# A gated cross-attention block on one Trainium2 core: the added rows of the last unit of the first two down parts stored from GpSimd's queue

## Chip, core and metric

The kernel runs on one core of one Trainium2 chip. The metric is the device time of one execution in microseconds (us); lower is better. Every launch includes all weight preparation.

## What is computed

The reference is a gated Flamingo layer in float32 on 2048 tokens (16 sequences of 128) of width 1024: a cross attention with 32 query heads and 8 key/value heads, then a gated feed-forward of hidden width 2752, each added to the stream behind a tanh gate.

```python
x = x + tanh(g_xattn[0]) * attention(layernorm(x), ctx, ctx, Wq, Wk, Wv, Wo)
h = layernorm(x).reshape(-1, 1024)
y = (silu(h @ W_gate.T) * (h @ W_up.T)) @ W_down.T
x = x + tanh(g_ffn[0]) * y
```

The change lies in the last line: the down projection and its addition to the stream.

## The kernel before

**Products.** Every float32 operand is split into a high and a low part (`split`, lines 112 to 115: a cast on ScalarE, a subtraction on VectorE), and a product is three matmuls for each slice of 128 of the inner dimension: high by high, high by low, low by high. A 2 by 2 block product is done with seven products of half size instead of eight. `still` (line 656) makes the sums of the stationary blocks and splits them into tiles `sta`, `stb`, `stc`, `std`; `premake`, `swap` and `casts` make the seven moving operands `m1` to `m7` (each a high tile such as `m1h` and a low tile such as `m1l`) from the weight.

**Down parts and units.** The hidden dimension of the down projection is done in three parts of 8, 8 and 6 tiles of 128 (`CHUNKS`). `Down(c, p)` is one unit: part `c`, 256 tokens number `p`, so 8 units a part and 24 in all. A unit runs the products in `ORDER = (1, 5, 6, 2, 7, 3, 4)`. Products 1, 6, 7 and 4 add up in one PSUM bank, and after each of them VectorE adds the bank to a row tile `c` (line 851), so TensorE may not write the next of them into the bank before VectorE has read the last.

**Row tiles.** A unit has four row tiles of 128 by 512, 256 KB each. `fetch` loads one from `x1d`, the stream kept in device memory, through ScalarE's queue (line 843), two products ahead of the product that first adds to it (1, 5, 6 and 4). After products 2, 7, 3 and 4 the row tile is complete and is stored (line 854): to `x1d` in the first two parts, to the output in the third. The tiles turn over in five buffers: a fetch can be issued only when the store that last used its buffer has landed. So the fetch for product 5 of a unit waits for the first store of the unit before it, the fetch for product 6 for the second, for product 4 for the third, and the fetch for product 1 of the unit after that for the fourth. ScalarE works in order: a fetch that waits holds the casts behind it.

**The turn of a part.** `swap` puts steps around the last unit of a part, unit 7, to bring in the next part's moving operands. In unit 7, after product 1 it splits `m1` and starts a weight load, after product 5 it splits `m5`, after product 6 it loads `m6` ready made (`bring`, line 962, two loads of 1 MB, `m6h` and `m6l`), and after product 4 it loads `m4` the same way. In unit 0 of the next part it splits `m2` after product 1, `m7` after product 5 and `m3` after product 6. In units 0 and 1 of each part the sums of `still` run on VectorE, in the others on GpSimd.

**Queues.** The program's order on each engine is the order in which Python emits it (a manual schedule). All loads and stores around the turn but the fetches go through SyncE's queue, one after another in order; GpSimd issues DMAs only for additions into memory (lines 922 and 1007), before the down parts. At the turn SyncE's order is: the weight load, `m6h`, `m6l`, the four stores of unit 7, `m4h`, `m4l`, and the load of hidden rows `raw` for two units ahead.

Of the kernel before, what the change touches and what calls it, by code (L numbers as in the profile page):

```python
# [17 lines left out]
P = 128  # L18
NTOK = 2048
# [17 lines left out]
CHUNKS = (range(0, 8), range(8, 16), range(16, 22))  # L37
# [17 lines left out]
def flamingo_kernel(ctx: ExitStack, tc: tile.TileContext, x, ctxt, gx, gf, wqkv, wo, wgu, wge, wd, out):  # L55
# [9 lines left out]
    nc = tc.nc  # L65
# [36 lines left out]
    od, rd, x1d = ([None] * (NTOK // P) for _ in range(3))  # L102
# [616 lines left out]
    class Gated:  # L719
# [22 lines left out]
        def done(self, p, ps, cols):  # L742
            c = self.c
            tt = nc.vector.tensor_tensor
            if p in (1, 5, 6):
                i = {1: 1, 5: 3, 6: 2}[p]
                if cols in (ALL, MOST):
                    self.room(i)
                nc.scalar.copy(c[i][:, cols], ps)  # L749
            elif p == 2:  # L750
                tt(c[1], ps, c[1], ALU.add)  # L751
            elif p == 7:
                tt(c[3][:, cols], c[3][:, cols], ps, ALU.subtract)
            elif p == 3:
                tt(c[2], ps, c[2], ALU.subtract)
                if self.amid:
                    self.amid()
                nc.scalar.activation(c[1], c[1], AF.Silu)
                nc.scalar.activation(c[2], c[2], AF.Silu)
                tt(c[2], c[2], c[3], ALU.mult)  # L760
                keep_hidden(self.g, self.f, c[2], 1)
            else:
                tt(c[1], ps, c[1], ALU.mult)
                keep_hidden(self.g, self.f, c[1], 0)
# [48 lines left out]
    class Down:  # L813
# [34 lines left out]
        def done(self, p, ps, _):  # L848
            y = self.y[self.PLACE[p]]
            g = tg[:, 2:3] if p in self.MINUS else tg[:, 1:2]  # L850
            nc.vector.scalar_tensor_tensor(y, ps, g, y, ALU.mult, ALU.add)  # L851
            if p in self.LAST:
                b, cols = self.row(p)
                nc.sync.dma_start(out[ts(b, P), cols] if self.c == len(CHUNKS) - 1 else x1d[b][:, cols], y)

    def run(units, cb, ready, steps, edge):

# [362 lines left out]
```

## Time and profile before

| | |
|---|---|
| median of 4 runs | 1839.84 us (1839.51 to 1842.57) |
| profiled execution | 1839.57 us |
| its span, first to last instruction | 1837.7 us |
| TensorE matmul busy | 1817.1 us, 99% of the span |
| VectorE / ScalarE / GpSimd busy | 1210.3 / 900.2 / 545.4 us |
| mean granted TensorE clock | 0.998 |
| line 854, stores to `x1d` | 64 of 256 KB |
| line 843, fetches from `x1d` | 96 of 256 KB |

The span is shorter than the execution by 1.9 us of start and end. In the profile, PE is TensorE, DVE is VectorE, ACT is ScalarE, POOL is GpSimd, SP is SyncE, and a "q" behind the name (SPq, ACTq, POOLq) is the engine's issuing of DMAs. The DMA queue q1 is SyncE's, q10 ScalarE's and q0 GpSimd's. The down parts run from about 1413 us to the end; the two turns that the change touches are near 1560 and 1715 us.

### The profile page before, as it was taken

What the parts mean: (1) busy time and instruction counts of PE and PEld (TensorE: products, weight loads), DVE (VectorE), ACT (ScalarE), POOL (GpSimd) and SP (SyncE); (2) the same over time, 40 slices, a digit from 0 to 9 for tenths busy, and PEclk for the clock granted to TensorE, in tenths of its full rate; (3) what the DMA queues carried; (4) which work ended last, traced back from release to release, by engine and by line L of the source; (5) the groups of instructions that cost most, each with busy time, mean ns of one, the idle gap of its engine ahead of it and who ended that gap; (6) DMA issues with size and microseconds to landing.
All of it is one profiled execution on the core that took longest, in us unless ns stands there. A gap on an engine that the chain in (4) does not pass through costs nothing.

```text
span 1837.7 us, 23463 instructions
## 1 busy us (share of the span) xinstructions
PE 1817.1 (99%) x8296; PEld 1493.4 (81%) x8296; DVE 1210.3 (66%) x1551; ACT 900.2 (49%) x1301; POOL 545.4 (30%) x372
## 2 busy tenths in 40 slices
PE   8999999999999999999999999999999999999999
PEld 7887877888887777787888888888888888788887
DVE  6757878678877777776668646355456646745765
ACT  4457787445678777776434434333334212312321
POOL 1136566221233333331021333244330231122021
PEclk9999999999999999999999999999999999999999
DMA  8699999774555445543674565675667566665764
GB/s 329 210 274 287 288 283 271 244 261 129 156 147 151 147 144 146 148 138 118 225 251 155 150 200 189 189 206 179 161 210 263 199 230 210 234 216 180 259 201 156
DMA packets 232565, 373.55 MB, mean 203 GB/s; under 512 B 38016, under 2 KB 124288, under 8 KB 227328
## 3 DMA queue, kind: packets, MB, share of 16 engines
q1 hardware_dynamic: 210400, 333.77, 55.3%
q10 hardware_dynamic: 14112, 25.17, 4.5%
q0 software_dynamic: 7936, 13.11, 4.4%
q8 instruction: 66, 1.08, 0.2%
q14 instruction: 51, 0.42, 0.1%
HBM read 247.99 MB, written 122.42 MB: 202 GB/s over the span
## 4 chain that ended last, share of the span: by engine, by line
PE 86%; DMA 5%; DVE 4%; ACT 2%; issue 1%; SPq 1%; POOL 0%; ACTq 0%; DVEq 0%; POOLq 0%
PE bx L707 35%; PE bz L707 17%; PE by L707 8%; PE bz L124 3%; PE bz L122 3%; PE bz L123 3%; PE bx L123 3%; PE bx L124 3%; PE bx L122 3%; DMA od<-os 2%; PE av L501 1%; PE av L500 1%; DMA qs<-qd 1%; PE by L472 1%; PE sc L472 1%
## 5 line engine op out<-in xcount | busy, mean ns | idle before, releaser
L483 POOL PARTITION_ALL_REDUCE mx<-pr x128 | 275.3, 2150 | 344.9 <-ACT pr L481 162.9
L674 POOL TENSOR_TENSOR sum<-raw 128x512 f32<-128x512 f32 (+1 forms) x37 | 48.0, 1297 | 479.4 <-DVE stc L115 479.4
L114 ACT CAST sta<-raw 128x1024 fp32r<-128x1024 f32 (+1 forms) x66 | 67.7, 1026 | 241.0 <-PE by L707 232.7
L707 PE MATMUL bz<-m5h,stb 128*128 128x512 f32 (+1 forms) x528 | 169.9, 383 | 0.0
L707 PE MATMUL bx<-m6h,stb 128*128 128x512 f32 (+1 forms) x528 | 169.6, 383 | 0.0
L707 PE MATMUL bx<-m7h,stc 128*128 128x512 f32 x512 | 168.9, 390 | 0.7 <-DVE c L851 0.7
L707 PE MATMUL bx<-m4h,std 128*128 128x512 f32 x512 | 169.0, 390 | 0.4 <-DVE c L851 0.4
L707 PE MATMUL by<-m2h,sta 128*128 128x512 f32 x512 | 168.5, 389 | 0.0
L707 PE MATMUL bz<-m3h,stc 128*128 128x512 f32 x512 | 168.5, 389 | 0.0
L707 PE MATMUL bx<-m1h,sta 128*128 128x512 f32 x512 | 168.4, 389 | 0.0
L751 DVE TENSOR_TENSOR c<-by,c 128x512 f32<-128x512 f32 x42 | 28.9, 687 | 144.1 <-issue 137.6
L144 POOL TENSOR_TENSOR rs__143<-ve,mhalf 128x1 f32<-128x1 f32 x32 | 29.3, 914 | 310.4 <-DVE nm L142 301.1
L495 DVE TENSOR_TENSOR pl<-pr,ph 128x512 fp32r<-128x512 f32 x128 | 120.1, 938 | 1.3 <-PE av L501 1.3
L851 DVE SCALAR_TENSOR_TENSOR c<-bx,tg,c 128x512 f32<-128x512 f32 x96 | 72.0, 750 | 66.8 <-PE bx L707 63.0
L707 PEld LDWEIGHTS bx<-m6h,stb 128*128 128x128 f32 x528 | 98.4, 188 | 20.1 <-ACT c L749 0.2
L707 PEld LDWEIGHTS bz<-m5h,stb 128*128 128x128 f32 x528 | 98.2, 188 | 20.2 <-DVE stb L115 0.5
L707 PEld LDWEIGHTS bx<-m4h,std 128*128 128x128 f32 x512 | 96.1, 188 | 22.2 <-DVE c L851 1.2
L707 PEld LDWEIGHTS bx<-m7h,stc 128*128 128x128 f32 x512 | 96.1, 188 | 22.0 <-issue 1.2
L707 PEld LDWEIGHTS by<-m2h,sta 128*128 128x128 f32 x512 | 96.1, 188 | 20.5
L707 PEld LDWEIGHTS bx<-m1h,sta 128*128 128x128 f32 x512 | 96.1, 188 | 20.4
L707 PEld LDWEIGHTS bz<-m3h,stc 128*128 128x128 f32 x512 | 96.1, 188 | 20.1
L486 DVE TENSOR_TENSOR pr<-pr,mx 128x512 f32<-128x512 f32 x128 | 87.6, 684 | 36.9 <-POOL mx L483 36.6
(400 smaller groups left out, 4636.7 us busy)
## 6 DMA issues: line engine op xcount, KB each, us to landing
raw<-in_wgu SPq DMA_DIRECT2D x42, 1024.0 KB, 6.5
x1d<-c SPq DMA_DIRECT2D x96, 256.0 KB, 2.8
c<-x1d ACTq DMA_DIRECT2D x96, 256.0 KB, 3.0
hd<-c SPq DMA_DIRECT2D x86, 256.0 KB, 2.2
od<-os SPq DMA_DIRECT2D x128, 160.0 KB, 4.1
qd<-e SPq DMA_DIRECT2D x32, 512.0 KB, 5.5
qs<-qd SPq DMA_DIRECT2D x64, 256.0 KB, 4.6
raw<-od SPq DMA_DIRECT2D x32, 512.0 KB, 5.2
```

The source lines that it names most:

```text
L114: nc.scalar.copy(h, src)
L122: nc.tensor.matmul(ps, lh, rh, start=first, stop=False)
L123: nc.tensor.matmul(ps, lh, rl, start=False, stop=False)
L124: nc.tensor.matmul(ps, ll, rh, start=False, stop=last)
L144: nc.gpsimd.tensor_tensor(rs, ve, mhalf, ALU.pow)
L472: nc.tensor.matmul(ss[n], ks[m][:, j, :], qs[m][:, ts(j, G)], start=True, stop=True)
L483: nc.gpsimd.partition_all_reduce(mx[n], pr[n], P, bass_isa.ReduceOp.max)
L486: nc.vector.tensor_tensor(pr[n], pr[n], mx.pop(n), ALU.subtract)
L495: nc.vector.tensor_tensor(pl[n], pr.pop(n), f32(ph[n]), ALU.subtract)
L674: lambda: tt(s1, a[1][0], a[1][1], sub),
L707: nc.tensor.matmul(ps, l_, r_, start=start and k == i == 0, stop=k == n - 1 and i == 2, skip_group_check=not start)
L851: nc.vector.scalar_tensor_tensor(y, ps, g, y, ALU.mult, ALU.add)
```

## The change

The four stores of unit 7 in the first and in the second part (8 of the 64 stores to `x1d`) are issued by GpSimd instead of SyncE. Nothing else is edited.

```diff
             if p in self.LAST:
                 b, cols = self.row(p)
-                nc.sync.dma_start(out[ts(b, P), cols] if self.c == len(CHUNKS) - 1 else x1d[b][:, cols], y)
+                final = self.c == len(CHUNKS) - 1
+                turn = self.p == NTOK // (2 * P) - 1 and not final
+                queue = nc.gpsimd if turn else nc.sync
+                queue.dma_start(out[ts(b, P), cols] if final else x1d[b][:, cols], y)
```

SyncE's order at a turn becomes: the weight load, `m6h`, `m6l`, `m4h`, `m4l`, `raw`. GpSimd gets four DMA instructions between the sums for unit 7 and the sums for unit 2 of the next part. The order on TensorE, VectorE and ScalarE is the same; the two fetches that wait for the first two stores now wait for GpSimd's transfers.

## The prediction

> **What bounds the kernel.** I read the page first, then the chain that ended last around the two turns, each engine's timeline there, and the DMA queues stretch by stretch.
>
> ```profile
> span 1837.7 us, 23463 instructions
> PE 86%; DMA 5%; DVE 4%; ACT 2%; issue 1%; SPq 1%; POOL 0%; ACTq 0%; DVEq 0%; POOLq 0%
> ```
>
> TensorE carries 86% of the chain. In the down parts it is nearly all of it, so a store can only matter where the chain leaves TensorE. The first turn is such a place. The chain there (start, us, what):
>
> ```profile
> 1554.58 2.73 PE by L707 x12
> ...
> 1557.34 0.76 DVE c L851
> ...
> 1558.11 8.74 DMA x1d<-c
> ...
> 1567.30 0.50 ACT std L114
> ...
> 1567.85 5.73 DMA c<-x1d
> 1573.57 2.20 DVE m7l L115
> ...
> 1582.91 5.78 PE bx L707 x24
> ```
>
> The first store of unit 7 takes 8.74 us to land. Until then ScalarE cannot issue the fetch for product 5 of the next unit (1566.88), and behind that fetch stand the `std` cast, the fetch for product 6 (1567.85) and the cast of `m2h` (1568.68). VectorE runs late, and TensorE's timeline shows what that costs:
>
> ```profile
> 1577.02 0.47 PE L707 MATMUL bx<-m7h,stc 128*128 128x512 f32 x1 [0.66 <-DVE c L851]
> 1582.91 0.50 PE L707 MATMUL bx<-m4h,std 128*128 128x512 f32 x1 [0.17 <-DVE c L851]
> ```
>
> How much is at stake follows from the pace. A product of a part of 8 tiles takes 2.72 us (12 matmuls). Product 2 of unit 7 starts at 1554.42, and product 4 of the next unit is ten products later: 1554.42 + 27.20 = 1581.62. It starts at 1582.91, so the first turn loses 1.29 us. At the second turn product 2 starts at 1708.20; four products of 2.72 and six of 2.04 (9 matmuls) give 1731.32, the row says 1731.70: 0.38 us. All that this change can remove is 1.67 us.
>
> **The change, part by part.** *SyncE's issues.* Eight issues of 0.32 us leave SyncE. Its own time is hidden (TensorE never waits for it here), but its order matters, on SyncE's timeline:
>
> ```profile
> 1554.61 0.32 SPq L962 DMA_DIRECT2D m6h<-m6d  x1
> 1554.98 0.42 SPq L962 DMA_DIRECT2D m6l<-m6d  x1
> 1558.11 8.90 SPq L854 DMA_DIRECT2D x1d<-c  x4
> 1567.06 0.42 SPq L962 DMA_DIRECT2D m4h<-m4d  x1
> ```
>
> The loads of `m4` stood behind the fourth store, whose addition on VectorE ends at 1566.66. Now they wait for their buffer alone, that is for the last matmul of product 4 (1565.09 plus 0.39): `m4h` goes out near 1565.6, 1.5 us earlier. At the second turn it is 1719.3 instead of 1720.43. Nobody gains: `m4` is first used at 1582.91, and `m4l`, issued at 1567.54, landed 9.2 us later, at 1576.7. But 2 MB of loads now stand ahead of fetches that were ahead of them or level. `raw` still waits for VectorE's `std` (1568.64) and goes out as before.
>
> *GpSimd's issues.* Four DMA instructions a turn. GpSimd's own rows give 1.27 to 1.30 us each for line 922 and 1.28 to 1.59 for line 1007, so 5 to 6 us a turn. They are free: GpSimd idles 54.46 us before the sums at 1587.12 and 48.67 us before those at 1735.11, and the last of the four can go out at 1566.7. Without that cover the sums would slip by some 5 us. The third and fourth stores release fetches issued at 1576.52 and 1581.22, ten and more us on, so those two cost nothing. The rows stored are read again a whole part later.
>
> *When the first store lands.* This decides. GpSimd has no plain store in the trace, so I bound it. The nearest of its transfers in size is one of 256 KB with nothing beside it, an addition in place:
>
> ```profile
> q<-q POOLq DMA_DIRECT2D x1, 256.0 KB, 4.7
> x1d<-c SPq DMA_DIRECT2D x1, 256.0 KB, 2.3
> ```
>
> Its 4.7 us against 2.3 us for a store from SyncE puts GpSimd's path at most 2.4 us longer. At the turn, though, neither row applies, since 2 MB of `m6` are in flight. What a queue of its own is worth there is shown by ScalarE's fetch issued at 1557.48: it was alone on q10 and took 8.4 us, hardly less than the store on q1. From 1557 to 1560 q10 moved nothing at all; then the queues took turns packet by packet. From 1562 to 1564:
>
> ```profile
> q1 hardware_dynamic: 65, 0.42, 67.5%
> q10 hardware_dynamic: 71, 0.15, 19.3%
> ```
>
> (packets, MB, share.) Packets are about equal, bytes are not: q1's are mostly 8 KB, the fetch's 2 KB. A third queue should get the same turns once `m6h` has passed. The lower end for the landing is 4.7 us (1562.8), the upper 8.74 + 2.4 = 11.1 us (1569.2). I take the 8.4 us of the fetch, the nearest row, because it shares instant, size and backlog: landing at 1566.5, 0.35 us earlier than now.
>
> The Trainium skill ("DMA: Bandwidth & Descriptors", section "Issuing engines are not separate DMA queues") says that DMAs of all engines run on the same 16 DMA engines and that spreading them only saves sequencer time. The 8.4 against 8.7 us agree in effect, and by that rule the change brings nothing. The same page (section "Queues, rings and completion order") has each DMA engine go round the queues packet by packet; the 71 against 65 packets agree, the empty q10 of the first 2.5 us does not, and no run here shows yet which of the two GpSimd's queue follows. By the second rule alone the store would land several us earlier and the 1.29 us of the first turn would go.
>
> *The fetch for product 5, first turn.* It is issued when the store lands, now near 1566.5 and behind `m4h` (1565.6) instead of ahead of it (1567.06). Ahead of it, it landed in 4.1 us; the fetch for product 6, issued at 1567.85 behind `m4h` and `m4l`, took 8.2 us. These are the bounds: 1570.6 and 1574.7. VectorE needs it at 1572.83. Only part of what delayed the row of 8.2 us applies (it also had the other fetch ahead of it), so I take the middle, 6.2 us: 1572.7, no cost and no gain. The ends: if the store lands before `m4h` is issued, the fetch goes out first, ScalarE and VectorE run some 1.5 us earlier and the whole 1.29 us go; if it lands no earlier than now and the fetch takes 8.2 us, it is there at 1575.1, VectorE's chain of `m7l`, product 6 and `m3l` (only 0.35 us of idle time in it) shifts by up to 2.25 us, and TensorE with it.
>
> *The second turn.* The first store landed in 5.4 us (issued at 1711.90) and is not on the chain: VectorE works without a gap from 1721.99 to 1731.6, started by TensorE's product 1. With 0.3 us less or up to 2.4 us more it lands by 1719.7. A fetch issued then has 3.9 us until VectorE's addition at 1723.66; the rows of this turn give 3.0 to 5.4 us, so its cost is 0 up to about 1 us. I take 0, and the 0.38 us stay.
>
> *Sum.* 1839.57 (profiled execution; span 1837.7 and 1.9 us around it) + 0 + 0 = 1839.6 us; 0.3 us under the median of 1839.84. Ends of this case: 1839.57 - 1.29 = 1838.3 and 1839.57 + 2.25 = 1841.8.
>
> **Rivals.** *The wait goes.* GpSimd's queue gets its turns at once, the store lands by 1565, the fetch passes ahead of `m4h`: 1838.3 us. For it: equal packets on q1 and q10. Against it: q10's silent start with 2 MB outstanding.
>
> *The store lands later than now.* The longer way through GpSimd adds to the backlog instead of hiding in it. With 11.1 us the store lands at 1569.2, 2.35 us later; the fetch goes out behind both loads of `m4` and, at 8.2 us, lands at 1577.4, 4.6 us after VectorE needs it. With 7.8 us at the second turn it is there at 1719.7 and, at 4.8 us (a fetch at 1727.58, beside the `m4` loads), lands 0.85 us late. Together 5.5 us: 1845.0 us. It decides from about 9.9 us for the landing at the first turn (9.9 - 8.74 + 2.25 = 3.4, plus some 0.3 at the second), where the loss passes 3.7 us. For it: GpSimd's 1 MB additions took up to 11.5 us, and one issued at 1106.28 amid other traffic 11.3 us. Against it: an addition reads its target too, and is four times the size.
>
> *The store's queue is no matter.* If the fetch still beats the loads, nothing changes: 1839.6 us, inside the forecast's range.
>
> **How the numbers follow.** The bound for a difference is 0.2%, 3.7 us, about what a measurement of this kernel can tell from no change. Forecast with its bounds (the indifferent queue included) 0.52; the wait goes 0.18; the store lands later 0.27, of which a tenth or so stays under 3.7 us; a gain over 3.7 us has no place in this profile, since both turns together lose 1.67 us, and gets 0.03 from the rest for what I cannot see. So faster 0.03, same 0.73, slower 0.24. The likeliest range is 1838.3 to 1841.8; for 8 in 10 it reaches down to 1837.9 (the whole 1.67 us) and up to the late store, 1845.0.
>
> **What would show it.** Right: the first `x1d<-c` of unit 7 on POOLq landing 7.5 to 9 us after VectorE's addition, `m4h` issued near 1565.6, the fetch for product 5 in 5 to 7 us, TensorE's product 4 of the next unit within 1 us of 28.5 us after product 2 of unit 7, no change at the second turn. Wrong: a landing under 6 us (gain) or over 10 us (loss), a wait of ScalarE of over 5 us ahead of `std`, or any move of TensorE away from the turns, for which I have no mechanism.

## The result and the profile after

| | median (lowest to highest) | runs |
|---|---|---|
| before | 1840.04 us (1835.69 to 1844.42) | 56 |
| after | 1842.62 us (1839.01 to 1846.87) | 36 |

The ratio is 1.0015, with a 95% interval of 1.0009 to 1.002: slower by about 2.6 us (1.7 to 3.7). That is under the 0.2% taken as the bound for one comparison, but with this many runs it stands clear of no change. The forecast was no change, 1839.6 us; the median lies 0.8 us above its likeliest range.

The profiled execution of after is one of the quickest (1839.04 us), so its span says nothing of the loss: it came to the first turn 2.5 us ahead of the profiled execution of before (product 2 of unit 7 starts at 1551.94 instead of 1554.42), and gave most of that back at the two turns. So I read each turn by itself. Its loss is the time from product 2 of unit 7 to product 1 of unit 1 of the next part, less the pace: 11 products of 2.72 us at the first turn (29.92), four of 2.72 and seven of 2.04 at the second (25.16). "+x" below means x us after the start of that product 2.

| | first turn | second turn |
|---|---|---|
| loss before | 1.46 us | 0.52 us |
| loss after | 2.89 us | 1.09 us |

The page of after, shares of the chain that ended last:

```profile
span 1837.3 us, 23467 instructions
...
PE 87%; DMA 5%; DVE 2%; ACT 2%; issue 2%; SPq 1%; POOL 0%; ACTq 0%; POOLq 0%; DVEq 0%
```

At this scale little moves. The chain of waits of after, around the first turn (start, us, what):

```profile
1559.04 5.55 DMA x1d<-c
1564.59 0.02 issue
1564.61 10.36 DMA c<-x1d
...
1575.09 0.10 DVE c L851
...
1575.76 2.28 DVE m3l L115
...
1581.88 5.75 PE bx L707 x24
```

Before, the chain went through the first store, of 8.74 us, and then the fetch for product 6 (its piece of 5.73 us in that chain is not the whole transfer, which took 8.2 us). Now it goes through the second store, of 5.55 us, and the same fetch, of 10.36 us. The store that the chain passes through is shorter, and the fetch is longer. Four timelines show why. First GpSimd, the two stores that release fetches:

```profile
1555.91 0.64 POOL L857 DMA_DIRECT2D x1d<-c  x1 [25.74 <-DMA q<-in_wd]
1559.04 0.55 POOL L857 DMA_DIRECT2D x1d<-c  x1 [2.49 <-DVE c L851]
```

Each issue takes 0.55 to 0.64 us and stands behind 2.4 us of idle or more. Then SyncE:

```profile
1552.13 0.32 SPq L965 DMA_DIRECT2D m6h<-m6d  x1
1552.50 0.42 SPq L965 DMA_DIRECT2D m6l<-m6d  x1
1563.03 0.32 SPq L965 DMA_DIRECT2D m4h<-m4d  x1
1563.40 0.43 SPq L965 DMA_DIRECT2D m4l<-m4d  x1
```

`m4h` goes out at +11.09 instead of +12.64, held only by TensorE's product 4. Then ScalarE, the fetches for products 5 and 6:

```profile
1563.47 0.33 ACTq L843 DMA_DIRECT2D c<-x1d  x1
...
1564.61 0.33 ACTq L843 DMA_DIRECT2D c<-x1d  x1
```

They go out 0.93 and 0.76 us earlier than before (+11.53 and +12.67 against +12.46 and +13.43), but now the first of them is 0.44 us behind `m4h`. What each transfer took, from the DMA issues (KB, us from issue to landing), the store first:

```profile
x1d<-c POOLq DMA_DIRECT2D x1, 256.0 KB, 7.5
...
c<-x1d ACTq DMA_DIRECT2D x1, 256.0 KB, 8.3
```

In before the same two took 8.74 and 4.1 us. The store gained 1.2 us, the fetch for product 5 lost 4.2. The fetch for product 6 stands behind it on ScalarE's queue: q10 moved 144 packets, one fetch's worth, from 1564.40 to 1570.52, and the other 144 from then to 1574.70. It took 10.4 us where before it took 8.2, the row of after first:

```profile
c<-x1d ACTq DMA_DIRECT2D x1, 256.0 KB, 10.4
...
c<-x1d ACTq DMA_DIRECT2D x1, 256.0 KB, 8.2
```

VectorE waits for the first with the addition of product 5, then for the second with the addition of product 6:

```profile
1571.91 0.75 DVE L851 SCALAR_TENSOR_TENSOR c<-bz,tg,c 128x512 f32<-128x512 f32 x1 [2.71 <-DMA c<-x1d]
...
1575.09 0.75 DVE L851 SCALAR_TENSOR_TENSOR c<-bx,tg,c 128x512 f32<-128x512 f32 x1 [0.23 <-DMA c<-x1d]
```

In before it came to the first addition without a wait, and earlier to the second:

```profile
1572.83 0.75 DVE L851 SCALAR_TENSOR_TENSOR c<-bz,tg,c 128x512 f32<-128x512 f32 x1
...
1576.12 0.75 DVE L851 SCALAR_TENSOR_TENSOR c<-bx,tg,c 128x512 f32<-128x512 f32 x1 [0.35 <-issue]
```

That wait of 0.35 us is put down to "issue", but it ends 0.08 us after the fetch for product 6 landed (1567.85 and 8.19 us). And TensorE waits for VectorE, in after:

```profile
1575.99 0.47 PE L707 MATMUL bx<-m7h,stc 128*128 128x512 f32 x1 [2.11 <-DVE c L851]
...
1581.88 0.50 PE L707 MATMUL bx<-m4h,std 128*128 128x512 f32 x1 [0.17 <-DVE c L851]
```

The idle time ahead of product 7 is 2.11 us where it was 0.66; the 1.45 us between them are the growth of the loss, 2.89 - 1.46 = 1.43. Both fetches have a part in it. The one for product 6 ended last: it landed at +23.03 instead of +21.62, 1.41 us later. But VectorE, held up by the one for product 5, was free only 0.23 us before that; with the old landing of product 6 it would still have come to that addition 1.2 us later than before (+22.92 against +21.70).

At the second turn the chain of waits of after goes through a weight load:

```profile
1718.59 7.55 DMA m4l<-m4d
1726.17 1.75 DVE m3l L115
...
1731.23 4.37 PE bx L707 x18
```

That step is put down to `m4l`, but VectorE's own row ahead of `m3l` names the fetch for product 6:

```profile
1725.50 0.75 DVE L851 SCALAR_TENSOR_TENSOR c<-bx,tg,c 128x512 f32<-128x512 f32 x1 [0.48 <-DMA c<-x1d]
```

This fetch went out at 1718.36, 0.14 us behind `m4h` (1718.22), and took 7.0 us. In before it was a microsecond ahead of `m4h` (+11.22 against +12.23) and took 3.0 us.

### The profile page after: what moved, and what is told of

Its sections match the earlier page's. It is cut to its first block, busy times and chain, and to the rows that moved or that the text cites. A ratio compares the mean times of both kernels' runs of the same rounds, so it can differ in the third digit from the quotient of the medians.

```text
span 1837.3 us, 23467 instructions
## 1 busy us (share of the span) xinstructions
PE 1814.5 (99%) x8296; PEld 1490.9 (81%) x8296; DVE 1211.8 (66%) x1551; ACT 900.5 (49%) x1301; POOL 551.8 (30%) x380
## 4 chain that ended last, share of the span: by engine, by line
PE 87%; DMA 5%; DVE 2%; ACT 2%; issue 2%; SPq 1%; POOL 0%; ACTq 0%; POOLq 0%; DVEq 0%
PE bx L707 35%; PE bz L707 17%; PE by L707 9%; PE bx L123 4%; PE bx L124 4%; PE bx L122 4%; PE bz L124 3%; PE bz L122 3%; PE bz L123 3%; DMA od<-os 2%; PE av L501 1%; PE av L500 1%; DMA raw<-in_wo 1%; PE by L472 1%; DMA c<-x1d 1%
```

## The experiments

Theory A is the order of the transfers. The four stores had held `m4h` and `m4l` back on SyncE's queue until VectorE's fourth addition. With the stores elsewhere these 2 MB go out about when the fetches do, and a fetch issued with or behind them takes twice as long. Theory B is the path of the store: a store through GpSimd lands late or at varying times, or its issues get in the way, and the loads of `m4` are no matter.

In this table "p5" and "p6" are the fetches for products 5 and 6, "→" the us from issue to landing, in the one profiled execution of each kernel. The ratio, with its 95% interval, comes from runs beside runs of before.

| kernel | ratio | first turn: `m4h`; p5; loss | second turn: `m4h`; p6; loss |
|---|---|---|---|
| before | | +12.64; +12.46 → 4.1; 1.46 | +12.23; +11.22 → 3.0; 0.52 |
| after | 1.0015 [1.0009, 1.002] | +11.09; +11.53 → 8.3; 2.89 | +11.07; +11.21 → 7.0; 1.09 |
| e1_first_two | 1.0001 [0.999, 1.0012] | +12.30; +10.82 → 3.9; 1.09 | +12.27; +11.21 → 3.1; 0.50 |
| e2_m4_ahead | 1.002 [1.0008, 1.0031] | +11.09; +11.68 → 7.4; 1.82 | +11.07; +11.21 → 5.7; 0.50 |
| e3_m4_late | 1.0002 [0.9993, 1.0011] | +12.97; +10.74 → 3.8; 0.05 | +12.74; +11.16 → 5.0; 0.51 |
| e5_m4_late_sync | 0.9998 [0.999, 1.0007] | +13.73; +11.52 → 4.1; 0.18 | +12.75; +11.24 → 3.4; 0.51 |
| e6_first_turn | 1.001 [1.0001, 1.0019] | +11.10; +10.52 → 3.8; 0.35 | +12.23; +12.55 → 6.7; 2.07 |
| e7_second_turn | 1.0017 [1.0008, 1.0025] | +12.26; +11.45 → 4.2; 0.84 | +11.07; +11.21 → 8.2; 2.24 |
| e8_half_ahead | 1.001 [1.0, 1.0019] | +11.10; +11.50 → 8.0; 2.62 | +11.07; +11.22 → 7.7; 1.73 |
| e9_last_two | 1.0029 [1.0019, 1.004] | +11.15; +11.56 → 8.0; 2.47 | +11.07; +11.49 → 6.9; 1.27 |
| e10_m4_gpsimd | 1.004 [1.0026, 1.0054] | +11.39; +11.68 → 8.6; 7.48 | +11.34; +11.21 → 3.5; 0.52 |
| e11_late_and_sums | 1.0008 [0.9999, 1.0017] | +14.71; +11.65 → 3.2; 0.13 | +13.33; +11.21 → 3.5; 0.55 |
| e12_changed_again | profile only | +11.10; +11.71 → 9.2; 3.72 | +11.08; +11.22 → 7.5; 1.54 |
| e13_changed_again | profile only | +11.09; +11.08 → 8.4; 2.92 | +11.07; +11.21 → 7.2; 1.30 |

**GpSimd's stores without the loads ahead.** Only the stores after products 2 and 7, the two that release fetches in the turn, are on GpSimd. The other two stay on SyncE and hold `m4` back as before.

```diff
-                queue = nc.gpsimd if turn else nc.sync
+                queue = nc.gpsimd if turn and p in (2, 7) else nc.sync
```

> Only the stores after products 2 and 7 go through GpSimd; those after 3 and 4 stay on SyncE, so the m4 loads again wait for the fourth store. Theory A (order lost: the m4 loads now reach the DMA engines ahead of the fetch for product 5, which then took 8.4 us instead of 4.1): the first store lands in 7 to 8 us as in the changed kernel, the fetch goes out ahead of m4h and lands in 3 to 5 us, the first turn loses 0 to 0.8 us (before 1.46, changed 2.89), the second about 0.5; the time is 0.5 to 1.5 us under before. Theory B (GpSimd's path itself is at fault: a third queue beside the others slows the fetches): those two stores are the ones that coincide with the m6 loads and the fetches, so the first turn loses 2.5 to 3 us as in the changed kernel and the time is 2 us over before.

The first store landed in 6.8 us, the fetch for product 5 went out 1.5 us ahead of `m4h` and took 3.9, the first turn lost 1.09 us, and the time is that of before. GpSimd's path costs nothing that can be told. I had expected less than 0.8 us of loss and a quicker time. What holds TensorE here is the fetch for product 6: issued at +12.05, 0.25 us ahead of `m4h` but behind the other fetch on its queue, it took 9.2 us.

**The loads ahead without GpSimd's stores.** From before, all stores on SyncE; in the down parts the loads of `m4` are issued ahead of the fourth store instead of behind it.

```diff
+                    if p == 4 and getattr(u, "ahead", None):
+                        u.ahead()
                     ...
-        u.after[4] = [lambda: bring("m4")]
+        if isinstance(u, Down):
+            u.ahead = lambda: bring("m4")
+        else:
+            u.after[4] = [lambda: bring("m4")]
```

> The kernel before, all stores on SyncE, but at the two turns the m4 loads stand ahead of the fourth store in SyncE's order, so they go out about 1 us earlier, as in the changed kernel, with nothing on GpSimd. Theory A: the first store lands as before (8.7 us), m4h goes out before the fetch for product 5, that fetch takes about 8 us, the first turn loses 3 to 4 us (before 1.46), the time is 1.5 to 3 us over before. Theory B: nothing of GpSimd's is in it, so the turns lose 1.4 and 0.5 us and the time is that of before.

SyncE's and ScalarE's timelines and the DMA issues of this kernel:

```profile
1565.88 0.32 SPq L964 DMA_DIRECT2D m4h<-m4d  x1
```

```profile
1566.47 0.33 ACTq L843 DMA_DIRECT2D c<-x1d  x1
```

```profile
c<-x1d ACTq DMA_DIRECT2D x1, 256.0 KB, 7.4
```

The loads go out at the time they have in after, the fetch 0.59 us behind them, and it takes 7.4 us. The ratio is that of after within the intervals, with no store on GpSimd's queue. Theory B falls here. The first turn was expected to lose 3 to 4 us and lost 1.82; the losses of this one profiled execution (2.32 us for both turns against 1.98) are smaller than its ratio would ask for, so the size rests on the ratio, and the mechanism on the order and the durations.

**GpSimd's stores, with the loads late.** From after; the loads of `m4` are issued after product 1 of the next unit, behind `raw`.

```diff
-        u.after[4] = [lambda: bring("m4")]
-        first.after[1] = [lambda: make("m2", 2)]
+        down = isinstance(u, Down)
+        if not down:
+            u.after[4] = [lambda: bring("m4")]
+        first.after[1] = [lambda: bring("m4")] * down + [lambda: make("m2", 2)]
```

> The changed kernel, all four stores on GpSimd, but at the two turns the m4 loads are put after product 1 of the next unit, behind the raw load, so that both fetches are ahead of them. Theory A: the fetches for products 5 and 6 land in 3 to 5 us, the first turn loses 0 to 0.8 us and the second 0.2 to 0.6, unless m4 itself comes too late for product 4 (it needs to land within about 13 us); the time is 1 to 1.5 us under before. Theory B: the stores are still GpSimd's, the first turn loses 2.5 to 3 us, the time is 2 us over before.

SyncE's timeline, and TensorE's row for product 4 of the next unit:

```profile
1570.60 0.32 SPq L827 DMA_DIRECT2D raw<-hd  x1
1571.01 0.38 SPq L965 DMA_DIRECT2D m4h<-m4d  x1
```

```profile
1585.29 0.39 PE L707 MATMUL bx<-m4h,std 128*128 128x512 f32 x1
```

No wait stands behind TensorE's row, and the first turn loses 0.05 us. The slowdown is gone with all eight stores still on GpSimd. The fetch for product 6 still takes 7.6 us, but lands at +19.60, before VectorE needs it. The gain of 1 to 1.5 us over before that I had expected does not show in the time.

**The same on SyncE.** The edit of the last experiment, made on before.

> The kernel before, all stores on SyncE, with the m4 loads after product 1 of the next unit as in the run with late m4. Theory A: the first store still lands in 8.5 us and holds ScalarE, the fetch for product 5 lands in 3 to 4 us as before, the one for product 6 in 3 to 5 instead of 8.2; what remains is the late cast of m2h, so the first turn loses about 1 us (before 1.46), the second 0.3 to 0.5; the time is 0 to 0.6 us under before. Theory B says nothing of the m4 loads: 1.4 and 0.5 us, the time of before.

0.18 us are lost at the first turn, where about 1 was expected, and the ratio is 0.9998. The profile is 1.29 us better than before at the two turns (0.69 against 1.98 us), but the time does not resolve it.

**One turn at a time.** The eight stores are split: only the first turn's, then only the second's.

```diff
-                turn = self.p == NTOK // (2 * P) - 1 and not final
+                turn = self.p == NTOK // (2 * P) - 1 and self.c == 0
```

> GpSimd's stores at the first turn alone, the second as before. The loss of a turn is counted from product 2 of unit 7 to product 1 of unit 1 of the next part, against TensorE's pace (29.92 and 25.16 us). Theory A (the m4 loads ahead of the fetches): the first turn loses 2 to 3 us as in the changed kernel (before 1.46), the second 0.5 as before; the time is 1 to 2 us over before. If instead the whole difference came from elsewhere (code or noise), both turns would show it in no order.

(`self.c == 1` in the second kernel.)

> GpSimd's stores at the second turn alone. Theory A: the first turn loses 1 to 1.5 us as before, the second 0.5 to 1.1 (there the fetch for product 5 is issued 1.8 us ahead of m4h and only that for product 6 falls behind it, 7 us instead of 3, with 0.5 us or less to pay); the time is 0 to 0.6 us over before.

Two of my expectations missed here. With only the first turn changed, that turn lost 0.35 us where 2 to 3 were expected. Its rows show why:

```profile
1566.64 0.32 SPq L965 DMA_DIRECT2D m4h<-m4d  x1
```

```profile
1566.06 0.33 ACTq L843 DMA_DIRECT2D c<-x1d  x1
```

```profile
c<-x1d ACTq DMA_DIRECT2D x1, 256.0 KB, 3.8
```

In this execution the store landed in 6.5 us, so the fetch was 0.58 us ahead of `m4h` instead of 0.44 behind, and took 3.8 us. The code at this turn is that of after: whether the store lands in 6.5 or in 7.5 us decides who is first. The same execution lost 2.07 us at its second turn, where the order is that of before: `m6l` took 9.7 us there, the store 7.8, the fetch for product 6 went out late (+12.55, behind `m4h`) and took 6.7 us.

With only the second turn changed, that turn lost 2.24 us, where at most 1.1 was expected: `m4h` at +11.07, the fetch 0.14 us behind, 8.2 us. Both halves are slower, the first barely clear of no change, so the loss is probably not one turn's alone. Their ratios add up to 1.0027, the whole gave 1.0015; the intervals are wide enough for both to hold, and I take no more from the sum.

**Half the load ahead.** From after, `m4h` stays after product 4, `m4l` moves behind product 1 of the next unit (`ks` says which of the two loads `bring` issues).

```diff
+        def bring(name, ks=(0, 1)):
                 ...
+        half = isinstance(u, Down)
-        u.after[4] = [lambda: bring("m4")]
-        first.after[1] = [lambda: make("m2", 2)]
+        u.after[4] = [lambda: bring("m4", (0,) if half else (0, 1))]
+        first.after[1] = [lambda: bring("m4", (1,))] * half + [lambda: make("m2", 2)]
```

> The changed kernel with half of the m4 loads taken out of the fetches' way: m4h as in it, m4l after product 1 of the next unit, behind the raw load. Theory A, by dose (2 MB ahead: 2.89 us lost at the first turn, none ahead: 0.05): 1 MB ahead of the fetch for product 5 lets it land in 5.5 to 7 us, and the first turn loses 0.3 to 1.5 us. A rival, that any transfer of SyncE's beside GpSimd's stores does it whatever its size, says 2.5 to 3 us.

I expected a fetch of 5.5 to 7 us; it took 8.0, and the first turn lost 2.62 us. With one load of 1 MB ahead the fetch is as slow as with two; that the size ahead does not count is not shown, since `raw` and `m4l`, 1 MB each, followed 1.8 and 2.2 us behind the fetch.

**The other half of the stores.** Only those after products 3 and 4 on GpSimd; the two that release the fetches stay on SyncE.

```diff
-                queue = nc.gpsimd if turn else nc.sync
+                queue = nc.gpsimd if turn and p in (3, 4) else nc.sync
```

> The other half of the change: the stores after products 3 and 4 through GpSimd, those after 2 and 7 on SyncE. They are the ones that stood between SyncE and the m4 loads. Theory A: the first store lands in 8 to 9 us as before, m4h goes out 11.1 us after product 2 (before 12.6), ahead of the fetch for product 5, which takes 7 to 8.5 us; the first turn loses 1.8 to 3.7 us, the time is 2 to 4 us over before, at least as much as in the changed kernel. Theory B (GpSimd's path is at fault): nobody waits for these two stores, so the time is that of before.

The stores that ScalarE waits for are back on SyncE, and the fetch still takes 8.0 us behind `m4h`. The ratio is 1.0029; the turns of its profile explain 1.76 us of these 5.3 (3.74 against 1.98), the rest I cannot place (the medians differ by 3.1 us; one run of the eleven, 1850.86, is far out). Read with e1_first_two: the two stores that moved the awaited transfer did no harm, the two that moved the obstacle did.

**The loads on a third queue.** From before, the stores on SyncE, the loads of `m4` issued by GpSimd.

```diff
-                nc.sync.dma_start(f32(z[:, :n]), made[name][:, k])
+                queue.dma_start(f32(z[:, :n]), made[name][:, k])
                 ...
+        other = nc.gpsimd if isinstance(u, Down) else nc.sync
-        u.after[4] = [lambda: bring("m4")]
+        u.after[4] = [lambda: bring("m4", other)]
```

> The kernel before, all stores on SyncE, but at the two turns the m4 loads go through GpSimd, where nothing holds them: they start about 11.1 us after product 2 of unit 7, ahead of the fetch for product 5. Asked: is a fetch slow behind them because SyncE's and ScalarE's queues share something, or because the DMA engines themselves are taken? If the engines (Theory A as it stands): the fetch for product 5 takes 6 to 8.5 us, the first turn loses 1.8 to 3.7 us, the time is 1.5 to 4 us over before. If only queues of the two sequencers stand behind each other: the fetch lands in 3 to 5 us and the turns lose as before or less, 0.5 to 1.5 and 0.5 us.

GpSimd's timeline, the fetch for product 5 in the DMA issues, and TensorE's product 7 of the next unit:

```profile
1565.81 0.62 POOL L962 DMA_DIRECT2D m4h<-m4d  x1 [33.16 <-PE bx L707]
```

```profile
c<-x1d ACTq DMA_DIRECT2D x1, 256.0 KB, 8.6
```

```profile
1581.31 0.77 PE L707 MATMUL bx<-m7h,stc 128*128 128x512 f32 x1 [4.93 <-DVE c L851]
```

The fetch was issued at 1566.10, 0.29 us behind `m4h`, and takes 8.6 us; the one for product 6 takes 13.4, and the first turn loses 7.48 us, where 1.8 to 3.7 were expected. Not all of that is the fetches'. The row of the stretch from 1579 to 1586 us (busy time of each engine, then the granted clock, the share of the DMA engines and GB/s) has TensorE's clock at 0.52:

```profile
1579.00:1586.00 7.00, 4.69 (x11) 3.76 (x12) 5.55 (x6) 0.56 (x1) 0.00 (x0) 0.52 0.12 43
```

Product 7, which falls into it, takes 5.04 us instead of 2.72, so 2.3 of the 7.48 us belong to the clock. No other profile has a lower clock in a turn. A fetch behind the loads is slow whichever of the two queues carries them. At the second turn the fetch for product 6 happened to go out 0.13 us ahead of the load, took 3.5 us, and that turn lost 0.52 us, as before.

**A version for speed.** e5_m4_late_sync, with the sums for unit 1 of each down part moved from VectorE to GpSimd, to give VectorE slack at the turn (`near = self.p < 1` for `self.p < 2`).

> A version meant to lose nothing: all stores on SyncE, the m4 loads after product 1 of the next unit, and the sums for unit 1 of every down part on GpSimd instead of VectorE (two of them, 1.1 to 1.4 us, stand in VectorE's chain ahead of the addition that lets product 4 begin). Theory A with what is left of VectorE's chain: the first turn loses 0 to 0.3 us, the second 0 to 0.3 (before 1.46 and 0.52), the time is 1.2 to 2 us under before. If GpSimd's slower sums come too late for the stb cast, the turn loses 1 us or more.

The turns lose 0.13 and 0.55 us, as hoped, but the ratio is 1.0008 and its interval leaves no room for a gain of more than 0.01%, where 1.2 to 2 us were expected. No version that I ran is measurably faster than before.

**The changed kernel twice more.** Unedited, one profile each, to see how often the fetch loses.

> The changed kernel, one more profiled execution, for the race at its first turn. Theory A: if the fetch for product 5 is issued before m4h (11.1 us after product 2) it lands in about 4 us and the first turn loses under 1 us; if after, in 7 to 8.5 us, and it loses 1.8 to 3 us. At the second turn the fetch for product 6 is always behind m4h: 5 to 8.5 us, 0.5 to 2.3 us lost.

> As the run before it, one more execution: the same two outcomes of the race at the first turn, and 0.5 to 2.3 us lost at the second.

It lost both times (9.2 and 8.4 us), the second time level with `m4h` within 0.01 us.

**All first turns together.** In seven profiles the fetch for product 5 went out 0.18 us or more ahead of `m4h` (before, e1, e3, e5, e6, e7, e11): 3.2 to 4.2 us. In seven it went out with it or behind (after, e2, e8, e9, e10, e12, e13): 7.4 to 9.2 us. There is no exception for this fetch, whichever queues carried store and loads. For the fetch for product 6 at the first turn the order against `m4h` does not decide in this way: it was ahead of it in e1, e3 and e5, by 0.25, 0.97 and 1.40 us, and still took 7.6 to 9.2 us, behind the other fetch and with `raw` or `m4h` following within a microsecond; only in e11, with 1.8 us to the next load, was it quick (3.7 us). And it is the one that ends last: in nine of the ten profiles in which TensorE waits for product 7 there, product 7 starts 0.97 to 1.03 us after this fetch has landed (in e2 1.46 us, where the other fetch holds VectorE). The fetch for product 6 at the second turn divides in the same way: ahead of `m4h` (before, e1, e3, e5, e10, e11) it took 3.0 to 5.0 us, behind it (all others) 5.7 to 8.2. For the size I take the changed order alone. It lost 2.89, 3.72, 2.92 and 0.35 us at the first turn (after, e12, e13, e6), 2.47 on the mean, and 1.09, 1.54, 1.30 and 2.24 us at the second (after, e12, e13, e7), 1.54 on the mean: 4.0 us, against 1.98 in the profile of before. The 2.0 us between them lie inside the measured 1.7 to 3.7. The old order varies too: counted with the first turn of e7 (0.84) and the second of e6 (2.07), which have it, its two means are 1.15 and 1.30 us, and 1.6 us are left, just under the interval.

## Why the prediction was wrong

*Where the kernel is bound: right.* The time was lost at the two turns, and TensorE's pace elsewhere did not change.

*GpSimd's issues: right in effect, wrong in price.* They were put at 1.27 to 1.59 us each by the rows of the additions; a plain store takes 0.54 to 0.64. Both are hidden.

*The landing of the first store: right.* 8.4 us were taken, 7.5 to 9 named as the sign; it was 7.5, in the later profiles of the same order 6.5, 7.7 and 7.1, two of them under the sign. The rival of the late landing, which decided from 9.9 us, did not come, though the time moved its way. The rival in which the wait goes happened in one profile of the four with the changed order at this turn, e6_first_turn, as it was written: a landing in 6.5 us, the fetch ahead of `m4h`, and 0.35 us lost instead of 1.46.

*`m4h` 1.5 us earlier: right*, to +11.09 from +12.64, and 2 MB now ahead of the fetches, as written.

*The fetches of the first turn: the term that failed.* For product 5 I had the bounds, 4.1 us ahead of the loads and 8.2 us behind them, and took 6.2 us, their middle, on the reason that only part of the delay applies. No run shows a middle for this fetch: 3.2 to 4.2 or 7.4 to 9.2 (the one for product 6 at the second turn does have 5.0 and 5.7). The term was 8.3 us, and by itself it brought VectorE to the addition of product 6 1.2 us later than before; e2_m4_ahead and e9_last_two give it nearly the same size (7.4 and 8.0) without GpSimd's stores in ScalarE's way. The fetch for product 6 got no price of its own at all: I used its 8.2 us as a bound for the other and left its landing where it was, though the 0.35 us of VectorE that I had read as idle were the wait for it. Behind a slower fetch on the same queue it took 10.4 us and landed 1.41 us later, and that wait ended last. Together they cost 1.43 us instead of nothing. By the fetch's issue, forecast 0.9 us behind `m4h` and found 0.44 behind, the row of 8.2 us was the one to take. With it and the landing taken at 1566.5 the fetch is there at 1574.7, 1.9 us after VectorE needs it; less the 0.35 us that VectorE had idle, the sum would have been 1839.57 + 1.5 = 1841.1 us. The sign that I named, TensorE's product 4 within 1 us of +28.5, was missed by 0.44 us: it started at 1581.88 - 1551.94 = +29.94.

*The second turn: overlooked.* I priced it at nothing after looking at the fetch for product 5 alone, which did land in time (2.9 us). The fetch for product 6 was the one at risk: before, it went out 1.0 us ahead of `m4h`, less than the 1.16 us by which `m4h` moves up (+12.23 to +11.07). Both numbers were in the profile of before. It took 7.0 us instead of 3.0 and cost 0.57 us here, more in the other profiles of the same order.

*The rules.* "DMA: Bandwidth & Descriptors", section "Issuing engines are not separate DMA queues", in the Trainium skill, holds that all queues end on the same DMA engines. That agrees with the 8.6 us of e10_m4_gpsimd against 8.3 of after. From it I had concluded that the change brings nothing; but the change also took away the order that one shared queue had given. The same page (section "Queues, rings and completion order") has each DMA engine go round the queues packet by packet, and I had worked out that by this rule alone the store would land several us earlier, its pieces of 2 KB taking turns with pieces of 8 KB. I had taken the page's packet for the profile's. The page's is typically some 9 to 17 descriptors, drained whole before the engine turns to the next queue; the profile's is at most one row of 2 or 8 KB, and a fetch is 144 of them, 9 for each of 16 engines. So the page does not promise an early turn, and no run here shows where its packets end. What after shows, in its DMA queues from 1564.2 to 1567 (packets, MB, share of 16 engines):

```profile
q1 hardware_dynamic: 77, 0.63, 82.4%
q0 software_dynamic: 14, 0.03, 3.8%
q10 hardware_dynamic: 16, 0.03, 3.4%
```

77 packets for SyncE's queue and 16 for ScalarE's, though its two fetches, issued at 1563.47 and 1564.61, wait there; only from 1567 to 1569 are they level, 80 and 79. So for some 3 us the queue that started first moves most of the packets, as q10's silence in the profile of before had hinted. I used that hint for the store and not for the fetch behind it.

*What stays open.* Moving the loads late mends the turns in every profile (0.05 to 0.18 us lost at the first), and yet the time of these versions is not measurably below before. Their profiles show no cost of it behind the first turn: 122.40 us lie between the two turns in all fourteen. The profiled executions come to the first turn at different times (1551.9 to 1558.8 us for the same product, counted from the start), which hides 1 us; that spread arises before about 900 us, ahead of the change. Nor did I find why e9_last_two is slower than its turns explain.

The granted clock was not tested as a part of the difference. Over the runs it is 0.9980 on the mean for after and 0.9984 to 0.9986 for the runs of before beside the experiments, and within after the longer runs mostly have the lower clock. 0.0005 of 1840 us would be 0.9 us of the 2.6. Time multiplied by clock is 1839.2 us on the mean for after and 1836.6 to 1837.5 for before, so by this estimate some 2 us remain that the clock does not explain. Whether the longer waits themselves lower the clock, as they may have done in e10_m4_gpsimd, is not shown. A sixth row buffer, which might take the wait off the fetch, was not tried.

## What to carry to other kernels

A queue that issues in order is also a schedule: before moving transfers off it, list what stood behind them, when it will go out now, and which small awaited transfer is issued within a microsecond of that. Where a small transfer and a large load come that close, price it by the row "behind the load" or "ahead of it", not by the middle, and give each its chance. Then follow what stands behind the small transfer on its own queue to its landing: here that one ended last. Do this for every such pair, at every place where the same step recurs.

## What the runs showed of the hardware

At the first turn the fetch for product 5, 256 KB, took 3.2 to 4.2 us when issued 0.18 us or more ahead of a 1 MB load and 7.4 to 9.2 us when issued level with it or up to 0.61 us behind it, with the load on SyncE's queue or on GpSimd's. The fetch next behind it on ScalarE's queue took 7.6 to 13.4 us, whether ahead of `m4h` or behind, in all profiles but e11_late_and_sums (3.7 us).

In the profile of e10_m4_gpsimd, TensorE stood idle for 4.93 us, and its granted clock was 0.52 from 1579 to 1586 us, a stretch that begins within that idle time; twelve matmuls took 5.04 us instead of 2.72.

A plain 256 KB store issued by GpSimd took 0.54 to 0.64 us of the engine, half of what the additions took, and the first of the first turn landed in 6.5 to 7.7 us, where SyncE's needed 7.7 to 8.7. It came in fewer packets: over the whole execution q1 has 1152 packets fewer for the eight stores, 144 each, and q0 has 640 more, 80 each. The totals before and after:

```profile
q1 hardware_dynamic: 210400, 333.77, 55.3%
q0 software_dynamic: 7936, 13.11, 4.4%
...
q1 hardware_dynamic: 209248, 331.67, 55.5%
q0 software_dynamic: 8576, 15.21, 4.7%
```
